# Two PSUM banks for the sums of y, with delta prepared in the one that is free, in a selective-scan kernel

## The chip, the cores and the metric

The kernel runs on one core of a Trainium2 chip. The metric is device time in microseconds, from the first to the last instruction of the program, as the median of several runs. An engine's share in the profile is taken over the span of one profiled execution, 5538.9 us.

## The reference

The input x is 4 images of 64 x 64 positions with 96 channels. Two layers run over it. Layer 0 normalises x in groups of three channels, projects it with signs only (weights and activations are replaced by their sign) to 192 channels xc and 192 channels z, runs a 3 x 3 convolution on the signs of xc, and applies SiLU; the result u has 192 channels and L = 4096 positions. Then comes a selective scan in K = 4 directions (rows, columns, and both backwards) with 16 states for each channel:

```python
x_dbl = jax.vmap(bilinear, ...)(xin, Wl, sl, bl)             # for each direction: dt (6), B (16), C (16)
dts = jax.vmap(bilinear, ...)(dts_in, Wd, sd, bd)            # 6 signs -> 192 channels
delta = jax.nn.softplus(delta + delta_bias)
def step(h, inp):
    ut, dt, Bt, Ct = inp
    dA = jnp.exp(dt[..., None] * A[None])
    h = dA * h + (dt * ut)[..., None] * Bt[:, :, None, :]
    y = jnp.einsum('bkdn,bkn->bkd', h, Ct)
    return (h, y)
```

The four directions of y are added, normalised over the channels, multiplied by SiLU(z) and projected with signs back to 96 channels. Layer 1 is attention without a softmax (so it collapses into small matrices summed over the image) and a feed-forward block with values rounded to 8-bit floats. What counts for this change is delta (softplus of a small projection), the scan, and the sum over the 16 states.

## The kernel before, in words

**Pieces.** The scan is cut into 1536 pieces (`Scans.pieces`): image b (4), direction e (4, in the order `KORD`), chunk ci of 1024 positions (4), group g of 32 channels (6), and quarter q of the 16 states (4). A piece is a tile of 128 partitions (32 channels x 4 states) by 1024 positions in float32. Its work, by engine:

- ScalarE, `decay` (L1231): dA = exp(delta x A), written into PSUM. There are two such tiles (pool `dA`, two banks each).
- GpSimd, `inject`: w = (delta x u) x B, four pieces ahead (`AHEAD`). The pool `w` has nine tiles.
- VectorE, `scan`: one scan instruction along the 1024 positions. It writes h over dA in PSUM or, if GpSimd is to make the product, into a tile `h` in SBUF.
- VectorE or GpSimd: the product h x C, over w. Which of the two is decided as the program is made: `Tally` adds up an estimate of each engine's work and `scan` gives the product to the one with less.
- ScalarE, `carry` (L1271): the last column of h is kept for the next chunk.
- TensorE, `reduce` (L1302, L1307): the sum over states, as a matmul with a constant of ones (`sum4`); eight pieces (two groups of channels) share one PSUM bank, tag `y`. With the last quarter of a group, earlier directions are added with a permutation (`back4`) or u with a diagonal (`dskip`).
- ScalarE, `evacuate` (L1316): copies the bank of sums to SBUF after eight pieces, and four stores follow.

**Order of a step.** The program is written in the order in which it is to run on each engine; no scheduler moves it. What is still chosen as it is built is which buffer of a pool a tile gets. In step i of `Scans.run` come: loads, carry(i-1), in every eighth step (i = 3 modulo 8) evacuate(i-4), decay(i+1), reduce(i-3), inject(i+4), a product that GpSimd still owes, scan(i), stores that are due (`Later.tick`), one stage of a preparation of delta, and one stage of the background work (`back`: the prologue of a later image, and the epilogue of an earlier one). Every engine works through its own queue in this order.

**Delta.** `prepare` makes softplus for 512 positions of 128 channels: eight small matmuls into a PSUM bank (tag `dps`), on ScalarE |t| and relu(t) (L1172, L1173), exp and ln (L1175, L1176) back into the same bank, a matmul that adds relu(t) (L1179), on VectorE the product with u, and on ScalarE a copy to SBUF (L1185). The results go to DRAM and come back, repeated over the states, with `load_dl`. One preparation begins in every eighth step, i = 0 modulo 8, and its stages lie in steps 0 to 5: matmuls; |t| and relu; exp and ln; relu added; product; copy. Three preparations run before the first scan, in tiles that the loop doesn't use yet.

**PSUM.** The eight banks are: four for the two dA tiles, one for sums of y, one for delta, two (`b0`, `b1`) for the background.

**Prologue.** For the group normalisation, the sums of x over all positions come from 64 matmuls, each with a tile of x (128 positions x 96 channels) as the weights and one column of ones moving (L510). The sums stand on 96 partitions, as the next matmul (`grp`, L516) needs them.

Of the kernel before, what the change touches and what calls it, by code (L numbers as in the profile page):

```python
# [53 lines left out]
def hybrid_kernel(ctx: ExitStack, tc: tile.TileContext, a: dict, out: bass.AP):  # L54
# [102 lines left out]
    def weights():  # L157
# [28 lines left out]
        def transposed(dst, srcs):  # L186

            count[0] += 1
            ps = p.ps.tile([128, 1024], BF16, name=f"tps{count[0]}", tag=("y", "dps")[count[0] % 2])
            at = 0  # L190
            for src in srcs:
                n, f = src.shape
                nc.tensor.transpose(ps[:f, at : at + n], src, identb[:n, :n])
                at += n
            nc.vector.tensor_copy(dst, ps[:f, 0:at], saturate=False if dst.dtype == F8 else None)
# [152 lines left out]
        nc.vector.tensor_copy(  # L348
            back4.rearrange("p (x d) -> p x d", x=4), ident.rearrange("p (x d) -> p x d", x=4)[:, ::-1, :]
        )  # L350
        ps = p.ps.tile([128, 512], F32, name="tpd", tag="dps")
        for g in range(3):
            for x in range(4):
                nc.tensor.matmul(
# [122 lines left out]
def prologue(c, b, xts=None):  # L477
# [5 lines left out]
    def f32(nm):  # L483
        return p.f.tile([128, 512], F32, name=f"{nm}_{b}", tag="f")
# [4 lines left out]
    with tc.tile_pool(name=f"xg_{b}", bufs=1) as xgp:  # L489
# [3 lines left out]
        with tc.tile_pool(name=f"cv_{b}", bufs=1) as cvp:  # L493
# [6 lines left out]
            if xts is None:  # L500
# [4 lines left out]
                load_x(c, b, xts)  # L505
                yield
                yield
            csum = bank("csum", 0)[0:96, 0:1]
            for i in range(NT):
                nc.tensor.matmul(csum, xts[i // 8][:, i % 8, :], c.ones1, start=(i == 0), stop=(i == NT - 1))  # L510
                if i % 8 == 7:
                    yield
            cs = f32("cs")[0:96, 0:1]
            nc.scalar.copy(cs, csum)
            gsum = bank("gsum", 1)[0:96, 0:1]
            nc.tensor.matmul(gsum, c.grp, cs, start=True, stop=True)  # L516
            yield
            negm = f32("negm")[0:96, 0:1]
# [578 lines left out]
class Scans:  # L1097
# [19 lines left out]
    def done(self, b, n):  # L1117

        return self.at > (b * NK + n) * NPC + SETTLE


    def load_signs(self, b, k):

# [6 lines left out]
    def prepare(self, spare=None):  # L1130

        nc, c, p = self.c.nc, self.c, self.c.p
        b, k, ci, part = self.todo.pop(0)
        nm = f"{b}_{k}_{ci}_{part}"

        at = 16 * (NCH - 1 - ci if k >= 2 else ci)
        if (b, k) not in self.gs:  # L1140
            self.load_signs(b, k)
        if (ci, part) == (NCH - 1, 0) and k != KORD[-1]:
            self.load_signs(b, KORD[KORD.index(k) + 1])
        ud = (c.utd if k % 2 else c.ud)[b].rearrange("h p (n l) -> (h p) n l", l=IW)
        if part != 1:
            u = spare[2] if spare else p.pu.tile([128, CH], F32, name=f"pu_{nm}", tag="pu")
            if part == 0:
                cuts = ((slice(0, 128), slice(0, 128), slice(at, at + 16)),)
            else:
                lines = [slice(at + 8 * x, at + 8 * x + 8) for x in range(2)]  # L1150
                cuts = [
                    (slice(64 * x, 64 * x + 64), slice(128, DN), lines[1 - x if k >= 2 else x]) for x in range(2)
                ]
            n = 16 if part == 0 else 8
            v = u[:, 0 : 64 * n].rearrange("p (n l) -> p n l", l=IW)
            for rows, chans, lines in cuts:
                nc.sync.dma_start(v[rows], ud[chans, lines])
            self.us = v[:, ::-1, ::-1] if k >= 2 else v
        gT = self.gs[b, k]
        uv = self.us[:, 8 * part : 8 * part + 8] if part < 2 else self.us  # L1160
        d = spare[0] if spare else p.pd.tile([128, 2, 512], F32, name=f"pd_{nm}", tag="pd")
        ps = spare[3] if spare else p.ps.tile([128, 512], F32, name=f"dps_{nm}", tag="dps")
        pv = ps.rearrange("p (c q s) -> p s q c", q=4, s=8)
        groups = ((0, 128, 0, part),) if part < 2 else ((0, 64, 128, 0), (64, 64, 128, 1))
        wd, c0 = (c.wdz, 32 * ci + 16 * part) if part < 2 else (c.wdy, 32 * ci)
        for s in range(8):
            nc.tensor.matmul(pv[:, s], wd[:, k, s], gT[:, :, c0 : c0 + 16], start=(s == 0), stop=(s == 7))  # L1167
        yield
        kind = part // 2
        sc, bi = c.pvd[:, kind, k : k + 1], c.dbias[:, kind, k : k + 1]  # L1170
        t = spare[1] if spare else p.pd.tile([128, 512], F32, name=f"sp_{nm}", tag="sp", bufs=1)
        nc.scalar.activation(d[:, 0], ps, AF.Abs, scale=sc, bias=bi)  # L1172
        nc.scalar.activation(t, ps, AF.Relu, scale=sc, bias=bi)  # L1173
        yield
        nc.scalar.activation(d[:, 0], d[:, 0], AF.Exp, scale=-1.0)  # L1175
        nc.scalar.activation(ps, d[:, 0], AF.Ln, bias=1.0)  # L1176
        yield

        nc.tensor.matmul(ps, c.ident, t, start=False, stop=True, skip_group_check=True)  # L1179
        yield  # L1180
        c.vec.tensor_tensor(
            d[:, 1].rearrange("p (i j) -> p i j", j=64), ps.rearrange("p (i j) -> p i j", j=64), uv, ALU.mult
        )
        yield
        nc.scalar.copy(d[:, 0], ps)  # L1185
        for x, (r0, n, d0, hf) in enumerate(groups):
            at = CH * ci + 512 * hf
            dst = c.dld[k][b][:, d0 : d0 + n, at : at + 512].rearrange("t d l -> d t l")
            then = (lambda: self.loaded.add((b, k, ci, part))) if x == len(groups) - 1 else None
            c.later.store(dst, d[r0 : r0 + n], after=1, then=then)  # L1190


    def load_bc(self, w, to, b, e, ci, q):
# [99 lines left out]
    def reduce(self, i):  # L1293

        c = self.c
        b, e, ci, g, q = self.pieces[i]
        if i % 8 == 0:
            self.ydone[i // 8] = c.p.ps.tile([128, 2, 256], F32, name=f"yp_{i}", tag="y")
        y, prod = self.ydone[i // 8], self.ins.pop(i)
        more = self.sums.pop(i // NQ, []) if q == NQ - 1 else []  # L1300
        for x in range(4):
            c.nc.tensor.matmul(  # L1302
                y[32 * x : 32 * x + 32, g % 2, :], c.sum4, prod[:, 256 * x : 256 * x + 256],
                start=(q == 0), stop=(q == NQ - 1 and not more), tile_position=(0, 32 * x),
            )
        for n, (src, w) in enumerate(more):
            c.nc.tensor.matmul(y[:, g % 2, :], w, src, start=False, stop=(n == len(more) - 1))  # L1307
# [15 lines left out]
    def run(self, back):  # L1323
        c, lanes, n = self.c, [], len(self.pieces)

        w = [c.p.w.tile([128, CH], F32, name=f"w_s{x}", tag="w") for x in range(7)]
        ps = [c.p.dA.tile([128, CH], F32, name=f"dA_s{x}", tag="dA") for x in range(2)]
        for x in range(3):
            half = slice(512 * (x % 2), 512 * (x % 2) + 512)
            lanes.append(  # L1330
                self.prepare((
                    w[x].rearrange("p (t l) -> p t l", t=2), w[3 + x // 2][:, half], w[5 + x // 2], ps[x // 2][:, half],
                ))
            )
        interleave(lanes)
        for q in range(NQ):
            self.load_bc(0, self.bt, 0, 0, 0, q)
            self.load_bc(1, self.ct, 0, 0, 0, q)
        while lanes:
            interleave(lanes)  # L1340
            c.later.tick()
        c.later.flush()
        self.load_dl(0)
        for m in (1, 2):
            self.load_dl(m)
        self.decay(0)
        for i in range(AHEAD):
            self.inject(i)
        for i in range(n):
            self.at = i  # L1350
            self.loads(i)
            if i % NQ == 1:
                while KORD[self.pieces[i][1]] == 2 and self.pieces[i][0] not in c.turned:
                    next(back)
                self.load_sums(i)
            if i >= 1:
                self.carry(i - 1)
            if i % 8 == 3 and i > 8:
                self.evacuate(i - 4)
            if i + 1 < n:  # L1360
                self.decay(i + 1)
            if i >= 3:
                self.reduce(i - 3)
            if i + AHEAD < n:
                self.inject(i + AHEAD)
            self.late_product()
            self.scan(i)
            c.later.tick()
            if i % 8 == 0 and self.todo:
                while (self.todo[0][0], self.todo[0][1] % 2) not in c.ready:  # L1370
                    next(back)
                lanes.append(self.prepare())
            interleave(lanes)
            next(back, None)
            if i > n - 64:
                next(back, None)
        self.late_product()
        for i in range(n - 3, n):
            self.reduce(i)
        self.evacuate(n - 1)  # L1380
        c.later.flush()
        self.at = 2 * n
# [76 lines left out]
```

## Time and profile before

Three runs took 5533.6, 5537.85 and 5543.78 us; the median is 5537.85.

| | busy us | share of the span | instructions |
|---|---|---|---|
| VectorE (DVE) | 5052.4 | 91% | 3237 |
| GpSimd (POOL) | 4994.2 | 90% | 2262 |
| ScalarE (ACT) | 3556.7 | 64% | 5564 |
| TensorE matmul (PE) | 3432.7 | 62% | 20197 |

The first scan starts 269 us after the first instruction and the last ends at 5421 us. In between, a piece takes 3.35 us on the mean. One scan takes VectorE 2.34 us and one product 1.23 us; a product takes GpSimd 2.35 us. A decay takes ScalarE 1.12 us.

How to read a line of groups: the line of the kernel, engine and operation, the tile written and those read, shapes and count; then busy us and mean ns of one; then the idle time of the engine just before such instructions, and what ended it. Line 401 is the helper that counts work, so there a group is told by its tiles. In a timeline each line is the start in us, how long it took, the engine, the line and the operation; in brackets stands how long the engine was idle before it and which instruction released it. Waits are listed as "who <- for whom: us in total, times, longest".

### The profile page before, as it was taken

The numbers are of one execution on the slowest core, as the hardware profiler recorded it, in microseconds if no ns is written. First come the engines' busy times: TensorE is split into PE (matmuls) and PEld (weight loads), VectorE is DVE, ScalarE is ACT, GpSimd is POOL, SyncE is SP. The second block draws the span as 40 slices with busy tenths as digits, with TensorE's granted clock in tenths as the row PEclk, the third lists the DMA queues.
The fourth block names the chain that finished last, engine by engine and source line by source line (L and its number), as shares of the span: only waits on it lengthen the run. The fifth ranks groups of instructions, "written<-read, shape, count | busy, mean of one in ns | idle before, by whom it ended". The sixth has DMA issues, their size and how long they took to land. (4 is left out here: it accounts for less than half of the span.)

```text
span 5538.9 us, 62371 instructions
## 1 busy us (share of the span) xinstructions
PE 3432.7 (62%) x20197; PEld 1356.7 (24%) x20197; DVE 5052.4 (91%) x3237; ACT 3556.7 (64%) x5564; POOL 4994.2 (90%) x2262
## 2 busy tenths in 40 slices
PE   6456665576557766577656766544676564444677
PEld 3222222222223222222222222211232121111223
DVE  3299999999999999899999999999999999999984
ACT  4467776777666667677766666755556775555554
POOL 2199999999999999899999999999999999999981
PEclk8667776678767876667777777766787766566778
DMA  4456666866766566666656566665666665665652
GB/s 78 118 179 198 207 194 193 258 193 199 220 203 194 194 205 199 218 217 207 205 193 212 185 200 210 212 211 191 210 215 186 191 205 198 205 208 190 207 159 60
DMA packets 613244, 1069.93 MB, mean 193 GB/s; under 512 B 225083, under 2 KB 343924, under 8 KB 611124
## 3 DMA queue, kind: packets, MB, share of 16 engines
q1 hardware_dynamic: 599428, 1065.88, 61.4%
q8 instruction: 159, 2.61, 0.2%
q10 hardware_dynamic: 13488, 0.07, 0.1%
q14 instruction: 169, 1.38, 0.1%
HBM read 833.20 MB, written 229.38 MB: 192 GB/s over the span
## 5 line engine op out<-in xcount | busy, mean ns | idle before, releaser
L401 POOL TENSOR_TENSOR w<-dl,bc 128x1024 f32<-128x1024 f32 x1536 | 3579.9, 2356 | 166.7 <-PE yp L1302 93.2
L1231 ACT ACTIVATE dA<-dl,anm 128x1024 f32<-128x1024 f32 x1536 | 1715.6, 1117 | 477.0 <-DVE w L401 291.5
L1302 PE MATMUL yp<-w,sum 128*32 128x256 f32 x12288 | 1261.6, 507 | 1083.2 <-ACT ys L1316 621.9
L401 DVE TENSOR_TENSOR_SCAN dA<-dA,cy,w 128x1024 f32<-128x1024 f32 x706 | 1654.4, 2343 | 94.7 <-ACT dA L1231 83.4
L401 POOL TENSOR_TENSOR w<-h,bc 128x1024 f32<-128x1024 f32 x596 | 1402.6, 2353 | 93.7 <-DVE h L401 85.2
L401 DVE TENSOR_TENSOR w<-dA,bc 128x1024 f32<-128x1024 f32 x940 | 1151.4, 1225 | 47.7 <-DVE dA L401 0.5
L401 DVE TENSOR_TENSOR_SCAN h<-dA,cy,w 128x1024 f32<-128x1024 f32 x446 | 1043.3, 2340 | 9.2 <-ACT dA L1231 8.7
L1302 PEld LDWEIGHTS yp<-w,sum 128*32 128x32 f32 x12288 | 308.0, 127 | 2136.9 <-issue 705.4
L1271 ACT COPY cy<-dA 128x1 f32<-128x1 f32 x707 | 110.8, 157 | 692.0 <-DVE w L401 690.7
L401 DVE TENSOR_TENSOR_SCAN dA<-dA,w 128x1024 f32<-128x1024 f32 x234 | 534.2, 2283 | 22.3 <-ACT dA L1231 18.0
L577 PE MATMUL cv<-tp,cw 96*96 96x512 fp8e5 x1152 | 359.9, 456 | 85.6 <-ACT r L627 70.5
L401 DVE TENSOR_TENSOR_SCAN h<-dA,w 128x1024 f32<-128x1024 f32 x150 | 341.8, 2279 | 24.4 <-POOL w L401 23.6
L1179 PE MATMUL dps<-sp,ident 128*128 128x512 f32 x378 | 356.8, 1043 | 0.0
L1307 PE MATMUL yp<-ya,back 128*128 128x256 f32 x576 | 237.8, 534 | 0.0
L577 PEld LDWEIGHTS <-cw 96*96 96x96 fp8e5 x1152 | 159.0, 146 | 277.5 <-issue 223.8
L1271 ACT COPY cy<-h 128x1 f32<-128x1 f32 x445 | 82.7, 186 | 145.6 <-DVE h L401 144.5
L847 PE MATMUL yc<-eys,mean 96*96 96x512 f32 x240 | 134.6, 713 | 33.3 <-DMA eys<-yd 14.5
L1307 PEld LDWEIGHTS yp<-ya,back 128*128 128x128 f32 x576 | 123.9, 248 | 127.8 <-issue 97.1
L1172 ACT ACTIVATE pd<-dps,dbias,pvd 128x512 f32<-128x512 f32 x189 | 143.8, 761 | 16.4 <-PE dps L1167 13.0
L1173 ACT ACTIVATE sp<-dps,dbias,pvd 128x512 f32<-128x512 f32 x189 | 144.7, 766 | 0.0
L401 DVE TENSOR_TENSOR pd<-dps,pu 128x512 f32<-128x512 f32 x189 | 127.6, 675 | 4.6 <-DMA dl<-dld 4.3
L1316 ACT COPY ys<-yp 128x512 f32<-128x512 f32 x192 | 111.7, 582 | 30.2 <-PE yp L1307 24.3
(282 smaller groups left out, 4017.6 us busy)
## 6 DMA issues: line engine op xcount, KB each, us to landing
dl<-dld SPq DMA_DIRECT2D x768, 512.0 KB
bc<-bcd SPq DMA_DIRECT2D x512, 512.0 KB
dld<-pd SPq DMA_DIRECT2D x126, 512.0 KB
yd<-ys SPq DMA_DIRECT2D x768, 64.0 KB
dld<-pd SPq DMA_DIRECT2D x126, 256.0 KB
ya<-yd SPq DMA_DIRECT2D x192, 128.0 KB
pu<-ud SPq DMA_DIRECT2D x32, 512.0 KB
pu<-utd SPq DMA_DIRECT2D x31, 512.0 KB
```

The costliest lines, as they stand in the source:

```text
L401: return getattr(self.eng, name)(out, *args, **kw)
L577: nc.tensor.matmul(ps, c.cw[:, j, t, 96 * h : 96 * h + 96], tpad[j][:, 8 * q + dy : 8 * q + dy + 8, dx : dx + IW], start=(j == 0 and t == ...
L847: self.c.nc.tensor.matmul(ps, w, x, start=(i == 0), stop=(i == len(pairs) - 1))
L1172: nc.scalar.activation(d[:, 0], ps, AF.Abs, scale=sc, bias=bi)
L1173: nc.scalar.activation(t, ps, AF.Relu, scale=sc, bias=bi)
L1179: nc.tensor.matmul(ps, c.ident, t, start=False, stop=True, skip_group_check=True)
L1231: c.nc.scalar.activation(t, self.dlt[i // NQ][0], AF.Exp, scale=c.anm[:, g, NQ * KORD[e] + q : NQ * KORD[e] + q + 1])
L1271: self.c.nc.scalar.copy(self.carries[g, q], h[:, CH - 1 : CH])
L1302: c.nc.tensor.matmul(y[32 * x : 32 * x + 32, g % 2, :], c.sum4, prod[:, 256 * x : 256 * x + 256], start=(q == 0), stop=(q == NQ - 1 and no ...
L1307: c.nc.tensor.matmul(y[:, g % 2, :], w, src, start=False, stop=(n == len(more) - 1))
L1316: c.nc.scalar.copy(t, y[:, :, ::-1] if k >= 2 else y)
```

## The change

There are five edits. The bank `dps` is given up, and the sums of y have two banks, `y0` and `y1`, in turn. A preparation of delta uses whichever of the two does not collect sums at the time (`bank`). For that it begins in steps 4 modulo 8, when the other bank has just been evacuated, and has to be done by step 10, as in step 11 (3 modulo 8) that bank takes new sums. Second, its ScalarE operations are spread out, one a step: matmuls; |t|; relu; exp; ln; relu added; product and copy, in steps 4 to 10. Third, in a step the decay now stands ahead of the evacuation. Fourth, as the preparations begin later in their eight steps, a fourth one runs before the first scan, and a store of delta is issued two ticks after it was asked for instead of one. Fifth, the sums of x are made with the ones as the weights, which stand, and four tiles of x (384 columns) moving: 16 matmuls, then a copy of the row, and four small matmuls that turn it onto 96 partitions while adding its four parts.

```diff
-            csum = bank("csum", 0)[0:96, 0:1]
-            for i in range(NT):
-                nc.tensor.matmul(csum, xts[i // 8][:, i % 8, :], c.ones1, start=(i == 0), stop=(i == NT - 1))
-                if i % 8 == 7:
+            csum = bank("csum", 0)[0:1, 0 : 4 * DM]
+            for i in range(0, NT, 4):
+                nc.tensor.matmul(
+                    csum, c.ones1, xts[i // 8][:, i % 8 : i % 8 + 4, :].rearrange("p i e -> p (i e)"),
+                    start=(i == 0), stop=(i == NT - 4),
+                )
+                if i % 8 == 4:
                     yield
+            row = f32("csr")[0:1, 0 : 4 * DM]
+            nc.scalar.copy(row, csum)
+            ps = bank("cst", 1)[0:96, 0:1]
+            for i in range(4):
+                nc.tensor.matmul(
+                    ps, row[:, DM * i : DM * i + DM], c.ones1[0:1, :], start=(i == 0), stop=(i == 3)
+                )
+            yield
             cs = f32("cs")[0:96, 0:1]
-            nc.scalar.copy(cs, csum)
...
+    def bank(self):
+        return max(0, self.at - 3) // 8 % 2
...
-        ps = spare[3] if spare else p.ps.tile([128, 512], F32, name=f"dps_{nm}", tag="dps")
+        ps = spare[3] if spare else p.ps.tile([128, 512], F32, name=f"dps_{nm}", tag=f"y{1 - self.bank()}")
...
         nc.scalar.activation(d[:, 0], ps, AF.Abs, scale=sc, bias=bi)
+        yield
         nc.scalar.activation(t, ps, AF.Relu, scale=sc, bias=bi)
         yield
         nc.scalar.activation(d[:, 0], d[:, 0], AF.Exp, scale=-1.0)
+        yield
         nc.scalar.activation(ps, d[:, 0], AF.Ln, bias=1.0)
         yield
...
         c.vec.tensor_tensor(
             d[:, 1].rearrange("p (i j) -> p i j", j=64), ps.rearrange("p (i j) -> p i j", j=64), uv, ALU.mult
         )
-        yield
         nc.scalar.copy(d[:, 0], ps)
...
-            c.later.store(dst, d[r0 : r0 + n], after=1, then=then)
+            c.later.store(dst, d[r0 : r0 + n], after=2, then=then)
...
-            self.ydone[i // 8] = c.p.ps.tile([128, 2, 256], F32, name=f"yp_{i}", tag="y")
+            self.ydone[i // 8] = c.p.ps.tile([128, 2, 256], F32, name=f"yp_{i}", tag=f"y{i // 8 % 2}")
...
+        u = c.p.pu.tile([128, CH], F32, name="pu_s", tag="pu")
+        for _ in self.prepare((w[7].rearrange("p (t l) -> p t l", t=2), w[4][:, 512:CH], u, ps[1][:, 512:CH])):
+            pass
...
+            if i + 1 < n:
+                self.decay(i + 1)
             if i % 8 == 3 and i > 8:
                 self.evacuate(i - 4)
-            if i + 1 < n:
-                self.decay(i + 1)
...
-            if i % 8 == 0 and self.todo:
+            if i % 8 == 4 and self.todo:
```

## The prediction, made before the result

> **What bounds the kernel now.** I read the page's table of engines first, then the same table for three stretches: up to the first scan, the loop over the 1536 pieces, and the tail.
>
> ```profile
> ## 1 busy us (share of the span) xinstructions
> PE 3432.7 (62%) x20197; PEld 1356.7 (24%) x20197; DVE 5052.4 (91%) x3237; ACT 3556.7 (64%) x5564; POOL 4994.2 (90%) x2262
> ...
> 0.00:269.00 269.00, 151.29 (x745) 87.85 (x746) 75.59 (x137) 121.16 (x198) 42.28 (x104) 0.79 0.44 95
> 269.00:5423.00 5154.00, 3200.21 (x19184) 1232.58 (x19183) 4925.79 (x3006) 3383.21 (x5278) 4948.66 (x2154) 0.71 0.64 201
> 5423.00:5539.00 116.00, 81.25 (x268) 36.26 (x268) 50.99 (x95) 52.31 (x88) 3.22 (x6) 0.78 0.22 64
> ```
>
> After the stretch and its length the columns are PE, weight loads, DVE, ACT, POOL. In the 5154 us of the loop VectorE is busy 4926 us and GpSimd 4949 us: both are nearly full, and the change alters the work of neither. Both programs, built, put 940 products on VectorE and 596 on GpSimd. What can move is idle time, so the next view is who VectorE waits for in the loop.
>
> ```profile
> DVE dA L401 <- ACT dA L1231: 101.3, 86, 5.5
> DVE h L401 <- POOL w L401: 23.6, 2, 14.4
> DVE g L401 <- PE sy L847: 19.7, 9, 4.6
> DVE h L401 <- ACT dA L1231: 9.3, 9, 3.1
> DVE dA L401 <- ACT cy L1271: 8.9, 12, 1.3
> ```
>
> Columns: total us, times, longest. All VectorE waits of the loop are 173 us (a further 54 us are gaps under 150 ns); 119.5 of them are for ScalarE (101.3 + 9.3 + 8.9), nearly always for the next decay. GpSimd as a releaser is two waits at the start. So **VectorE sets the time, and ScalarE's lateness is its only large wait.** GpSimd's own waits (93.6 us for sums, 85.2 us for scans) are slack while VectorE doesn't wait for it. The timeline shows how a decay comes late:
>
> ```profile
> 2412.25 2.34 DVE L401 TENSOR_TENSOR_SCAN h<-dA,cy,w 128x1024 f32<-128x1024 f32 x1
> 2412.73 0.15 ACT L1271 COPY cy<-dA 128x1 f32<-128x1 f32 x1
> 2414.62 1.12 ACT L1231 ACTIVATE dA<-dl,anm 128x1024 f32<-128x1024 f32 x1 [1.74 <-DVE h L401]
> ...
> 2415.84 2.36 DVE L401 TENSOR_TENSOR_SCAN dA<-dA,cy,w 128x1024 f32<-128x1024 f32 x1 [1.25 <-ACT dA L1231]
> ...
> 2418.26 0.58 ACT L1316 COPY ys<-yp 128x512 f32<-128x512 f32 x1
> ...
> 2418.74 1.12 ACT L1231 ACTIVATE dA<-dl,anm 128x1024 f32<-128x1024 f32 x1
> ...
> 2419.96 2.36 DVE L401 TENSOR_TENSOR_SCAN dA<-dA,cy,w 128x1024 f32<-128x1024 f32 x1 [0.43 <-ACT dA L1231]
> ```
>
> Two kinds. First, the decay at 2414.62 was given the PSUM banks that the running scan still reads, though the other pair was free; it starts when that scan ends, and VectorE then stands 1.25 us. Second, the decay at 2418.74 stands behind the evacuation at 2418.26. The built program says how often the first happens: 73 decays lie in the banks of the piece just ahead. Numbering the trace's scans in order, VectorE idles 84.9 us before those 73 (1.16 each). Of the other idle for ScalarE (37.7 us), 16.2 us fall on pieces 4 modulo 8, whose decay follows an evacuation, 4.7 on pieces 3 modulo 8, about 10 on pieces 0 modulo 8, where ScalarE waits for squares of the epilogue.
>
> **What the Trainium skill says.** (1) "PSUM — Partial Sum Buffer", section Engine vs sequencer instructions: ScalarE's and VectorE's queues are strict FIFO. The trace agrees: at 2412.9 ScalarE has ready work behind the decay and sits 1.74 us. (2) Same page, PSUM bank collisions raise a hardware error: instructions of different engines on one bank are kept apart by a dependency, a read from a read too. The trace agrees: the carry copy, which needs only the scan, waits 690.7 us in all for the product that reads the same tile. (3) "Perfetto Trace Analysis", Optimization Strategy: a repeating bubble on the full engine can mean too little PSUM for the next tile; the 1.25 us is one. (4) Same page, Optimizing Scalar/DVE Operations: breaking up work on an unsaturated engine that causes bubbles elsewhere may help. That speaks for the change; ScalarE is 66% busy in the loop (3383/5154).
>
> **The change part by part.** The rows that price it:
>
> ```profile
> L401 DVE TENSOR_TENSOR pd<-dps,pu 128x512 f32<-128x512 f32 x189 | 127.6, 675 | 4.6 <-DMA dl<-dld 4.3
> L1316 ACT COPY ys<-yp 128x512 f32<-128x512 f32 x192 | 111.7, 582 | 30.2 <-PE yp L1307 24.3
> L1185 ACT COPY pd<-dps 128x512 f32<-128x512 f32 x189 | 109.2, 578 | 3.7 <-DVE pd L401 3.7
> L510 PE MATMUL csum<-ones,xt 128*96 128x1 f32 x256 | 42.6, 297 | 18.2 <-DMA xt<-in_x 18.2
> ```
>
> (a) Decay ahead of the evacuation, one ScalarE operation of delta a step. Both take work out from in front of a decay. At most the 16.2 and 4.7 us above go; nothing else in the 37.7 us comes from these operations. I take -21.
>
> (b) The copy of delta now stands in the same step as the VectorE multiplication, where before a step lay between. They read one bank, so the copy waits for the multiplication, and the multiplication runs after that step's scan and product. Queued behind the copy are the step's background operations, a carry copy and the decay of piece 4 modulo 8, for which VectorE waits next. From the start of the multiplication: it ends after 0.7, copy 0.5, background B, carry 0.2, decay 1.1, 0.1 to the scan: 2.6 + B. VectorE needs that decay after 0.6 + 2.25 = 2.85 if piece 3 modulo 8 has its product on GpSimd, 4.0 if not. So the stall is B - 0.23 or B - 1.38. The built program has 188 such copies in the loop; 102 of the pieces after them have their product on GpSimd (before, pieces 3 modulo 8 had 68, as the load count that picks the engine sees the multiplication first). Pairs of background operations (B near 1.1 to 1.3) are common. Summing B by the rows' means over the built order, less what falls together with (c), gives 17 us in 35 places. Bounds: 0 (ScalarE always early) and 50 (other lateness adds). I take +17.
>
> (c) Which banks a decay gets. In the changed program 91 decays lie in the banks of the piece just ahead instead of 73; the 18 more are nearly all at 4 modulo 8 (28 against 11). 18 x 1.16 = +21. Bounds 0, if ScalarE would have been late there anyway, and 18 x 1.7 = 31 (the mean at 1 modulo 8).
>
> (d) Two banks for sums. TensorE's first matmul of eight waited 621.9 us in all for the evacuation. It now waits for the copy of (b), in the bank that delta just used, and that copy ends about 0.5 us later in the step than the evacuation did. So this wait is renamed, not removed. Behind it are TensorE's sums and background matmuls; GpSimd waits for the sums to give buffers back, VectorE does not wait for GpSimd. I take 0; a bound of +30 if GpSimd's waits grow by a third and reach VectorE.
>
> (e) Start. A fourth delta is prepared before the loop: 3 us of ScalarE and a multiplication that waits for a load queued behind six others, and the first decay queues behind its copy. I expect the first scan up to 6 us later. It is hidden: GpSimd's six first products run from 266.6 to 280.4, and the third scan waits 9.2 us for GpSimd anyway. One multiplication less in the loop: -0.7. Column sums: 64 matmuls took 10.3 us (32.7 to 43.0, clock 1.00). The 16 new ones move 384 columns; a float32 matmul of 512 columns has two passes, and eight such passes in a row took 3.67 us at full clock with 0.59 us for one, so 0.44 apart ((3.67 - 0.59)/7); 384 columns give 0.33, and 16 x 2 x 0.33 = 10.6. Nothing is won; a row copy, four small matmuls and one more step come after: +1.5 on the path to the first scan. For images 1 to 3 this lies in the background.
>
> Longer lead of the delta store and the other bank tags: nothing, as VectorE waits for that load only once (4.3 us).
>
> Sum: -21 + 17 + 21 + 0 - 0.7 + 1.5 = +19, so 5538 + 19 = **5557 us**.
>
> **The rivals.** *Smoother ScalarE pays (5512).* (b) is hidden and the 18 extra bank clashes fall where ScalarE is late anyway; then -21, and 5 of the remaining 17 us go too: -26. For: ScalarE has a third of its time free. Against: the built order puts the copy between two decays. *It cancels (5538).* Gains of (a) against half of (b) and (c). For: the three terms are of one size. Against: nothing in particular. *GpSimd becomes the bound (5585).* (d) lengthens its waits so far that injections reach VectorE late; +30 and the +19. For: 93.6 us of such waits now. Against: four pieces of lead, and no such VectorE wait after the start.
>
> **How the numbers follow.** Main case (5545 to 5575) 0.45, faster 0.20, cancelling 0.25, GpSimd 0.10. Slower by over 0.2% means above 5549: all of GpSimd's and nearly all of the main case, 0.55; within 0.2% 0.25; faster 0.20. For eight in ten I go from 5510 (just below the faster rival) to 5592 (both upper bounds partly in).
>
> **What would show it.** VectorE's waits for the decay rise from 119.5 to about 140 us, gathered on pieces 4 modulo 8; the copy of delta waits for the multiplication on ScalarE (3.7 us before) by over 100 us; TensorE's wait for the evacuation turns into one for that copy of about the same total; VectorE's busy time stays within 5 us; the first sum group (third scan) starts within 4 us of 282.8. The prediction is wrong if the waits before scans fall under 100 us, or if GpSimd shows up as a releaser of scans beyond the start.

## The result, and the profile after

The changed kernel takes 5563.18 us, the median of four runs (5557.92 to 5568.8); the kernel before took 5539.91 us in four runs (the three above and one more). The ratio is 1.0043, 95% interval 1.0026 to 1.0061: slower by 23 us, a small loss, but one that the measurement tells from nothing.

The table of engines of the changed kernel comes first, with two groups from the list of costly ones.

```profile
PE 3508.2 (63%) x20037; PEld 1353.2 (24%) x20037; DVE 5054.7 (91%) x3237; ACT 3546.9 (64%) x5568; POOL 4996.7 (90%) x2262
...
L1319 PE MATMUL yp<-w,sum 128*32 128x256 f32 x12288 | 1320.2, 525 | 806.8 <-ACT pd L1202 343.2
...
L1202 ACT COPY pd<-dps 128x512 f32<-128x512 f32 x188 | 110.2, 586 | 445.9 <-DVE pd L401 445.9
```

The first of these two groups in the kernel before (the second stands in the prediction, as L1185):

```profile
L1302 PE MATMUL yp<-w,sum 128*32 128x256 f32 x12288 | 1261.6, 507 | 1083.2 <-ACT ys L1316 621.9
```

VectorE's and GpSimd's busy times have moved by 2.3 and 2.5 us (5052.4 and 4994.2 before), ScalarE's by 10. TensorE's rose by 75 us with fewer instructions; a sum took 507 ns and now takes 525, on an engine that is 63% busy. So the 23 us are not work of a full engine but idle time between its instructions. The copy of delta (L1202) is what stands out: it takes about as long as before, 586 ns (578 before), but ScalarE now stands 445.9 us in front of it, where it stood 3.7.

Next, VectorE's waits in the loop of the changed kernel (total us, times, longest).

```profile
DVE dA L401 <- ACT dA L1248: 104.1, 93, 3.0
DVE w_s L401 <- DMA pu_s<-utd: 20.4, 1, 20.4
DVE h L401 <- ACT dA L1248: 15.2, 18, 2.2
...
DVE dA L401 <- ACT cy L1288: 9.7, 7, 2.1
DVE pd L401 <- PE dps L1197: 8.7, 3, 4.8
```

The three rows for ScalarE give 104.1 + 15.2 + 9.7 = 129.0 us (119.5 before). The rows for TensorE grew too, so these three alone are not the whole difference. For that I cut the time in three at the third scan and at the last one, and within the loop added up all of VectorE's waits over 150 ns:

| us | third scan starts | loop, third scan to last | VectorE's waits in it | loop without them | last scan to the end |
|---|---|---|---|---|---|
| before | 282.8 | 5138.7 | 163.7 | 4975.0 | 117.4 |
| after | 276.3 | 5164.2 | 188.3 | 4975.9 | 122.5 |
| difference | -6.5 | +25.5 | +24.6 | +0.9 | +5.1 |

The loop grew by 25.5 us, and VectorE's waits in it by 24.6. In all kernels below the loop without its waits stays between 4965 and 4978 us, so VectorE's waits are what every experiment changes. The last column lies between 117.4 and 122.8 us in all thirteen kernels (122.5 in e1, 117.7 in e6, which differ only in the order of a step), so its 5.1 us are not put down to the change.

By the engine that the profile names as the releaser, ScalarE has 126.3 us of these waits before and 137.6 after, TensorE 26.6 and 40.1. So about half of the added waiting is for TensorE, 8.7 us of it in three waits for the matmul that adds relu to delta (the last row above), for which VectorE did not wait at all before.

Where the waits fall, by numbering the scans ("idle at 4 modulo 8" is VectorE's idle time in front of the scans of pieces 4, 12, 20 and so on): 73 pieces lay in the PSUM banks of the piece just ahead (a bank clash, below), with 84.9 us of idle in front of their scans; now 91 do, with 102.9 us. All other scans at 4 modulo 8 had 16.2 us and now have 9.1; those at 3 modulo 8 fell from 4.7 to 1.1.

On TensorE the first of eight sums waited 621.9 us for the evacuation (L1302 above). In the changed kernel that wait has two names:

```profile
PE yp L1319 <- ACT pd L1202: 343.2, 101, 6.3
...
PE yp L1319 <- ACT cy L1288: 117.9, 33, 6.0
```

Together 461 us, a quarter less.

At the start, the timeline of the changed kernel shows the fourth delta in front of the first scans.

```profile
268.43 0.69 DVE L401 TENSOR_TENSOR w_s<-dA_s,pu_s 128x512 f32<-128x512 f32 x1 [20.37 <-DMA pu_s<-utd]
269.15 0.59 ACT L1202 COPY w_s<-dA_s 128x512 f32<-128x512 f32 x1 [16.77 <-DVE w_s L401]
...
270.87 4.47 DVE L401 TENSOR_TENSOR_SCAN h<-dA,w 128x1024 f32<-128x1024 f32 x2 [1.74 <-ACT dA L1248]
276.33 2.29 DVE L401 TENSOR_TENSOR_SCAN h<-dA,w 128x1024 f32<-128x1024 f32 x1 [1.00 <-POOL w L401]
```

VectorE stands 20.4 us for the load of u, the first scan starts at 270.9 instead of 269 us, and the third one waits a last microsecond for GpSimd, where it waited 9.2: the delay is hidden, as GpSimd's first products still end later than it, but little room is left.

### The profile page after: what moved, and what is told of

Same layout as the page of the kernel before. It is cut to its first block, busy times and chain, and to the rows that moved or that the text cites. A ratio compares the mean times of both kernels' runs of the same rounds, so it can differ in the third digit from the quotient of the medians.

```text
span 5563.1 us, 61882 instructions
## 1 busy us (share of the span) xinstructions
PE 3508.2 (63%) x20037; PEld 1353.2 (24%) x20037; DVE 5054.7 (91%) x3237; ACT 3546.9 (64%) x5568; POOL 4996.7 (90%) x2262
## 5 line engine op out<-in xcount | busy, mean ns | idle before, releaser
L401 POOL TENSOR_TENSOR w<-dl,bc 128x1024 f32<-128x1024 f32 x1536 | 3583.3, 2362 | 161.0 <-PE yp L1319 81.9
L1319 PE MATMUL yp<-w,sum 128*32 128x256 f32 x12288 | 1320.2, 525 | 806.8 <-ACT pd L1202 343.2
L401 DVE TENSOR_TENSOR_SCAN dA<-dA,cy,w 128x1024 f32<-128x1024 f32 x705 | 1652.3, 2344 | 97.8 <-ACT dA L1248 78.5
L1197 PE MATMUL dps<-sp,ident 128*128 128x512 f32 x376 | 343.7, 1012 | 233.5 <-ACT dps L1194 233.5
L1202 ACT COPY pd<-dps 128x512 f32<-128x512 f32 x188 | 110.2, 586 | 445.9 <-DVE pd L401 445.9
L1324 PE MATMUL yp<-ya,back 128*128 128x256 f32 x576 | 215.4, 491 | 1.2 <-DMA ya<-y 1.1
L1197 PEld LDWEIGHTS dps<-sp,ident 128*128 128x128 f32 x376 | 85.3, 283 | 369.9 <-ACT dps L1194 310.1
L1183 PE MATMUL dps<-gT,wdz 128*128 128x64 fp8e5 x1000 | 117.8, 320 | 41.1 <-DMA gT<-gTd 21.2
```

What stands on the lines that cost most here:

```text
L401: return getattr(self.eng, name)(out, *args, **kw)
L1319: c.nc.tensor.matmul(y[32 * x : 32 * x + 32, g % 2, :], c.sum4, prod[:, 256 * x : 256 * x + 256], start=(q == 0), stop=(q == NQ - 1 and no ...
```

## The experiments

Two things had to be taken apart: whether the loss comes from the extra bank clashes (term c of the prediction) or from the copy behind its multiplication (term b), and whether the parts meant as gains (terms a and d) gain anything. Each ratio is to the kernel before, run beside it on the same chip. There were three batches (e1 to e4, e5 to e8, e9 to e11), in which the kernel before took 5540.8, 5536.5 and 5538.7 us, so a difference of medians between two batches holds up to 4 us that belong to no edit. The last column is from one profiled execution of each kernel (163.7 us before, 188.3 in the changed kernel).

| label | built from | what is different | us | ratio, 95% interval | VectorE's waits in the loop, us |
|---|---|---|---|---|---|
| e1 | before | dA tiles take turns | 5485.1 | 0.9902 (0.9887 to 0.9917) | 117.0 |
| e2 | after | dA tiles take turns | 5501.7 | 0.9937 (0.9924 to 0.9949) | 124.4 |
| e3 | e2 | multiplication a step ahead of the copy | 5455.7 | 0.9850 (0.9836 to 0.9863) | 88.9 |
| e4 | e2 | evacuation ahead of the decay | 5527.1 | 0.9974 (0.9965 to 0.9983) | 150.0 |
| e5 | e3 | one ScalarE operation a step again | 5446.7 | 0.9840 (0.9825 to 0.9854) | 82.1 |
| e6 | e1 | decay ahead of the evacuation | 5489.7 | 0.9913 (0.9900 to 0.9927) | 122.3 |
| e7 | after | multiplication a step ahead of the copy | 5508.9 | 0.9951 (0.9938 to 0.9963) | 139.1 |
| e8 | before | new column sums | 5539.8 | 1.0008 (1.0000 to 1.0017) | 160.7 |
| e9 | e2 | sums and delta each in one bank | 5516.4 | 0.9955 (0.9943 to 0.9968) | 138.9 |
| e10 | e5 | sums and delta each in one bank | 5457.8 | 0.9854 (0.9839 to 0.9869) | 95.4 |
| e11 | e1 | copy in the step of its multiplication | 5494.3 | 0.9921 (0.9907 to 0.9934) | 122.5 |

**The bank clashes: e1 and e2.** The two dA tiles get a tag each, so that a piece can't be given the banks of the piece ahead: 73 and 91 clashes become none (the few other users of the pool get one of the two tags as well). Nothing else of the order changes. The same edit was made on the kernel before (e1) and on the changed one (e2).

```diff
-dA=pool("dAp", 2, space=PSUM)
+dA=pool("dAp", 1, space=PSUM)
...
-        t = c.p.dA.tile([128, CH], F32, name=f"dA_{i}", tag="dA")
+        t = c.p.dA.tile([128, CH], F32, name=f"dA_{i}", tag=f"dA{i % 2}")
```

> The kernel before, with the two dA tiles forced to take turns (a tag for even pieces, one for odd), so that no decay gets the banks that the running scan reads; before, 73 did. Theory A (VectorE's wait for a late decay is the time, and a bank clash costs it 1.16 us): the 85 us of idle before those scans go, so 5540 becomes 5455 to 5480, and VectorE's waits for decays in the loop fall from 119 to 25 to 50 us. Theory B (a clash falls where ScalarE is late anyway, or GpSimd's waits for sums set the time): little or nothing, 5525 to 5545.

> The changed kernel with the same forced turns (91 clashes to none). Theory A: 103 us of idle go, so 5563 becomes 5460 to 5485, and against the kernel before with forced turns it is within 10 us, because what then remains of the change is -21 for the earlier decay and the split, +17 for the copy behind the multiplication. Theory B: stays at 5550 to 5565. Theory C (the sums' wait on the copy of delta is the loss): still 20 to 30 us above the kernel before with forced turns.

Measured: -54.8 us on the kernel before, -61.5 on the changed one: a clear gain in both, but e1 stays above the 5480 and e2 above the 5485 us that theory A allowed, and e2 is 16.6 us above e1, not within 10. VectorE's waits for decays in e1 are 64.6 us, not 25 to 50. The gap was not for lack of PSUM, as point (3) of the prediction took it: the same two tiles, in turns, do without it. In the kernel before 84.9 us stood in front of the clashing scans and 49.7 in front of all others, 134.6 together; in e1 78.5 us are left. So 29 of the 85 us came back as other lateness, most of it at 1 modulo 8 (2.1 us at scans without a clash, now 15.4) and 4 modulo 8 (16.2, now 22.7). A clash is worth 54.8/73 = 0.75 and 61.5/91 = 0.68 us, not the 1.16 us that stand in front of it in the trace. By the medians the extra clashes of the changed kernel cost 61.5 - 54.8 = 6.7 us; by VectorE's waits (188.3 - 124.4 less 163.7 - 117.0) they cost 17.2. The first is a difference of three ratios, each known to 7 to 10 us either way, and the second rests on one execution of each kernel, so their cost stays open between nothing and some 20 us. What is left between the two kernels without clashes, 16.6 us, must come from the other edits.

**The copy behind its multiplication: e3 and e7.** The multiplication goes one step ahead of the copy again; to keep the copy in step 10, |t| and relu share a step. On e2 (e3), and on the changed kernel as it is (e7).

```diff
         nc.scalar.activation(d[:, 0], ps, AF.Abs, scale=sc, bias=bi)
-        yield
         nc.scalar.activation(t, ps, AF.Relu, scale=sc, bias=bi)
...
             d[:, 1].rearrange("p (i j) -> p i j", j=64), ps.rearrange("p (i j) -> p i j", j=64), uv, ALU.mult
         )
+        yield
         nc.scalar.copy(d[:, 0], ps)
```

> The changed kernel with forced turns, and the copy of delta one step behind its multiplication again (for which |t| and relu(t) share a step as before). If the copy behind the multiplication costs the predicted 17 us: 10 to 20 us less than the changed kernel with forced turns, and ScalarE's wait for the multiplication before that copy (446 us) falls under 50. If it costs nothing: within 5 us of it, or slower because the sums now wait a step longer for the bank.

> The changed kernel as it is (buffers chosen as built), with only the copy of delta put one step behind its multiplication and |t| and relu(t) in one step. Its build has 65 bank clashes instead of 91. With forced turns this step took 46 us off. Theory A: 40 to 60 us off 5563, so 5503 to 5525, which is faster than the kernel before; VectorE's waits fall from 189 to about 140. If the copy behind the multiplication costs only the 17 us predicted: 5530 to 5545 with the 26 clashes.

Measured: e3 is 46.0 us faster than e2, e7 54.3 us faster than the changed kernel (e7 also has 65 clashes instead of 91, an estimated 18 us at the 0.7 us above, so e3 is the cleaner of the two). For e3 10 to 20 us were expected; e7 is as expected, VectorE's waits in it too (139.1 us). ScalarE's wait for the multiplication falls from 449.5 us in e2 to 1.6 in e3. One edit of two lines takes the changed kernel from slower than before to faster. The same place of the program in both traces shows how. First e2, ScalarE and then VectorE, at the piece where three background operations (B = 1.8 us) follow the copy:

```profile
1969.01 0.59 ACT L1202 COPY pd<-dps 128x512 f32<-128x512 f32 x1 [2.87 <-DVE pd L401]
1969.49 0.59 ACT L1082 CAST h<-hp 128x512 f16<-128x512 f32 x1
1970.11 0.72 ACT L1083 ACTIVATE h<-h,b1q 128x512 f16<-128x512 f16 x1
1970.74 0.61 ACT L1085 ACTIVATE h<-h 128x512 fp8e5<-128x512 f16 x1
1971.26 0.14 ACT L1288 COPY cy<-dA 128x1 f32<-128x1 f32 x1
1971.43 1.12 ACT L1248 ACTIVATE dA<-dl,anm 128x1024 f32<-128x1024 f32 x1
```

```profile
1968.29 0.68 DVE L401 TENSOR_TENSOR pd<-dps,pu 128x512 f32<-128x512 f32 x1
1968.89 2.34 DVE L401 TENSOR_TENSOR_SCAN h<-dA,cy,w 128x1024 f32<-128x1024 f32 x1
1972.64 2.36 DVE L401 TENSOR_TENSOR_SCAN dA<-dA,cy,w 128x1024 f32<-128x1024 f32 x1 [1.41 <-POOL w L401]
```

ScalarE has nothing to do for 2.87 us, because its queue is headed by a copy that has to wait. Then it has 3.5 us of work before the decay is done (1969.01 to 1972.55), and VectorE could use that decay 2.3 us after the end of the multiplication, when the scan in between ends. The bracket names GpSimd as the last releaser, but the decay ends at 1972.55 and the scan starts at 1972.64: it is the decay that came last. Now e3, ScalarE at the same piece:

```profile
1943.42 1.12 ACT L1248 ACTIVATE dA<-dl,anm 128x1024 f32<-128x1024 f32 x1
1944.47 0.58 ACT L1202 COPY pd<-dps 128x512 f32<-128x512 f32 x1
1944.95 0.58 ACT L1082 CAST h<-hp 128x512 f16<-128x512 f32 x1
...
1946.80 1.11 ACT L1248 ACTIVATE dA<-dl,anm 128x1024 f32<-128x1024 f32 x1
```

```profile
1945.96 2.33 DVE L401 TENSOR_TENSOR_SCAN dA<-dA,cy,w 128x1024 f32<-128x1024 f32 x1
```

The copy goes right behind the decay, and VectorE's scan of that piece has no idle in front of it. Over the loop, idle at 4 modulo 8 falls from 30.6 to 6.3 us; VectorE's waits for delta's relu matmul fall from 9.5 to 0.7, idle at 2 modulo 8 from 9.8 to 2.4; at 3 modulo 8 it rises from 2.5 to 12.3. The edit also moves exp, ln, the relu matmul and the multiplication one step earlier, so not all of the 46 us need come from the copy's wait: what stands behind the copy, at 4 modulo 8, is 24 us.

**The same term in the kernel before: e11.** On e1 the step between multiplication and copy is taken out.

```diff
             d[:, 1].rearrange("p (i j) -> p i j", j=64), ps.rearrange("p (i j) -> p i j", j=64), uv, ALU.mult
         )
-        yield
         nc.scalar.copy(d[:, 0], ps)
```

> The kernel before with dA tiles that take turns (5485.1 us) and one more edit: the copy of delta in the step of its multiplication (steps 4 modulo 8 instead of 5). This is the second term of the prediction alone. By the prediction's size: 5502. By the size that the changed kernel showed (46 us): 5525 to 5535, ScalarE's copy waiting some 400 us for the multiplication, VectorE's idle gathered behind it. Rival (in the kernel before ScalarE's step has room there, and the cost comes only with the other edits): 5485 within 6 us.

ScalarE's waits in e11:

```profile
ACT pd L1184 <- DVE pd L401: 408.5, 186, 6.7
```

ScalarE's wait is nearly as long as in the changed kernel (445.9), and yet the kernel is only 9.2 us slower than e1, by the medians (the intervals overlap). The idle behind the copy is there: at 6 modulo 8, whose decay follows the copy here, it rises from 4.8 to 25.1 us. But the other scans lose 6.5 us of idle (73.7 to 67.2) and other instructions of VectorE 8, so that all its waits in the loop grow by 5.5 us only. So the stall itself has the size of e3's at 4 modulo 8 (20 and 24 us); what becomes of it depends on what else is late. Of the sizes expected of the whole, the 46 us of e3 is excluded here; neither the predicted 17 us nor no cost at all fits the medians well, but the intervals exclude neither. In the changed kernel the late copy also holds up the decays and TensorE's work of the steps next to the evacuation; which of these accounts for the rest of the 46 us was not taken apart.

**Decay ahead of the evacuation: e4 and e6.** Taken back on e2 (e4, below), and done alone on e1 (e6, the same lines the other way round).

```diff
-            if i + 1 < n:
-                self.decay(i + 1)
             if i % 8 == 3 and i > 8:
                 self.evacuate(i - 4)
+            if i + 1 < n:
+                self.decay(i + 1)
```

> The changed kernel with forced turns, and the evacuation ahead of the decay as before (edit 3 undone). If that order was worth the predicted 16 us: 5 to 16 us slower than the changed kernel with forced turns, with the new idle of VectorE on pieces 4 modulo 8. If ScalarE has time there now that delta is spread: within 5 us.

> The kernel before with forced turns, and of the change only the decay ahead of the evacuation. VectorE idles 22.7 us on pieces 4 modulo 8 in the kernel before with forced turns (5485). Theory A: most of it goes, 5462 to 5475. If the wait of the sums for the evacuation mattered more (the evacuation comes 1.1 us later in the step): the same or slower, 5480 to 5500.

In the changed kernel the order is worth 25.4 us, more than the 5 to 16 expected: without it idle at 4 modulo 8 is 54.6 us instead of 30.6. In the kernel before it is worth nothing (5489.7 against 5485.1, with intervals that overlap), which was the second of the two expectations. There idle at 4 modulo 8 does fall, from 22.7 to 10.3 us, but with one bank for the sums the evacuation now comes a decay later, and the sums wait for it: 763.7 us on TensorE where e1 has 586.7. Delta's matmul stands behind the sums, so VectorE waits for that:

```profile
DVE pd L401 <- PE dps L1179: 18.0, 14, 5.0
```

In e1 that wait is 4.4 us. So the gain of 12 us on one wait is given back by others. That it is the single bank which makes the difference between e4 and e6 is read from these waits; no run of one bank with the order of e4 shows it.

**Two banks for the sums: e9 and e10.** Sums always in one bank and delta always in the other, as before; on e2 (e9) and on e5 (e10).

```diff
-tag=f"y{1 - self.bank()}"
+tag="y1"
...
-tag=f"y{i // 8 % 2}"
+tag="y0"
```

> The second kernel of these experiments (the changed one with dA tiles that take turns, 5501.7 us) with the two banks' turns taken back: sums of y always in one bank, delta always in the other, as in the kernel before; every other edit stays. Theory of the prediction (the second bank only renames TensorE's wait): 5502 within 10 us, the wait of the first sums named after the evacuation again, about 600 us. Rival one (the second bank is what makes the decay ahead of the evacuation harmless): the sums wait for an evacuation that is now behind the decay, delta's matmul queues behind them, 5515 to 5530. Rival two (the sums suffer from waiting for the late copy, which no longer gates them here): 5475 to 5490.

> The fastest kernel so far (5446.7 us: turns for the dA tiles, the copy one step behind its multiplication, one ScalarE operation a step) with sums always in one bank and delta always in the other. If the second bank is worth nothing by itself: 5447 within 8 us. If it is what lets the decay go ahead of the evacuation: 5465 to 5485, with VectorE's waits for delta's matmul on TensorE above 10 us (0.7 in the kernel with the late copy).

TensorE's longest wait in e9 is again that for the evacuation:

```profile
PE yp L1319 <- ACT ys L1333: 813.0, 165, 9.2
```

Without turns TensorE's wait for the evacuation is 813.0 us in e9 and 820.1 in e10, where e2 has 328.3 us for the copy of delta and 124.4 for a carry copy. The time grows by 14.7 and by 11.1 us; each pair's intervals just overlap, but both point one way, and VectorE's waits in the loop grow by 14.4 and 13.3 us. By the ratios, which take out the differences between batches, it is 10 and 8 us. So e9 falls in the range of its first rival and e10 between its two expectations. Neither goes the way that was expected: VectorE's wait for delta's matmul stays at 8.0 us in e9 (9.5 in e2) and at 0.9 in e10. What rises is GpSimd's wait for sums to free its buffers (66.3 us in e2, 100.3 in e9; 47.0 in e5, 64.7 in e10) and idle at 6 modulo 8 (4.7 and 16.4; 9.7 and 19.4); how the one leads to the other is not shown. So the second bank is worth some 8 to 15 us once the decay goes ahead of the evacuation: probably more than a renaming, but not what everything hangs on.

**One ScalarE operation a step: e5.** On e3, |t| and relu each get a step again, and a preparation begins one step earlier to have time for both.

```diff
         nc.scalar.activation(d[:, 0], ps, AF.Abs, scale=sc, bias=bi)
+        yield
         nc.scalar.activation(t, ps, AF.Relu, scale=sc, bias=bi)
...
-            if i % 8 == 4 and self.todo:
+            if i % 8 == 3 and self.todo:
```

> The changed kernel with forced turns of the dA tiles, the copy of delta one step behind its multiplication, and still one ScalarE operation of delta a step: the preparation begins one step earlier, in steps 3 modulo 8, right after the evacuation of that bank. Theory A (late decays are the time): the 12 us of idle that came on pieces 3 modulo 8 in the variant where |t| and relu(t) share a step go, so 5440 to 5455. If one operation a step is worth nothing by itself: 5456 within 5 us.

9.0 us less than e3 by the medians and 5.5 by the ratios, with intervals that overlap. VectorE's waits in the loop fall from 88.9 to 82.1 us, which agrees with it. But the idle at 3 modulo 8 that was to go falls only from 12.3 to 10.2 us, and at 6 modulo 8 it rises from 1.9 to 9.7; what is gained lies at 1 and 5 modulo 8 and in front of VectorE's other instructions. Most likely a small gain; it is not shown beyond doubt. This kernel beats both: 1.6% less than the kernel before, and by the medians 116 us less than the changed one. It has all five edits of the change, with the multiplication a step ahead of its copy and the dA tiles in turns.

**Column sums alone: e8.** The diff is that of the change (its first part), on the kernel before.

> The kernel before with only the column sums of x made the new way; its build has 75 bank clashes (before 73). Expected: 5532 to 5548, with the bias for the signs of x ready at 45 us as before (7.6 us of matmuls for 10.3, but a copy, small matmuls and a step more). If standing ones are a gain of their own: ready 3 us earlier.

No difference (1.0000 to 1.0017). The 64 matmuls took 10.34 us and the 16 new ones take 7.48, but the row copy and the four small matmuls after them take the 3 us back: in the kernel before the value that the image waits for (`negm`) comes 12.4 us after the first of these matmuls (32.7 to 45.1 us), in e8 12.9 (31.4 to 44.3).

## Why the prediction was right

Direction and size were right: +19 us forecast, +23 measured, all of it in VectorE's waits. The place was right in part: the forecast had the loss in waits for late decays on ScalarE, and about half of it is in waits for TensorE. That the sum came so near is luck, for its terms missed by more than the sum did, in both directions. (As written they add up to +17.8, not +19.) With e1, e2, e6 and e9 the 23.3 us divide as follows, by the medians and by VectorE's waits in the loop:

| part | kernels compared | medians, us | VectorE's waits, us |
|---|---|---|---|
| extra clashes | before, e1, e2, after | +6.7 | +17.2 |
| decay ahead of the evacuation | e1, e6 | +4.7 | +5.3 |
| place and spread of the preparation, its copy, the fourth preparation, the later store, the column sums | e6, e9 | +26.7 | +16.5 |
| second bank in turns | e9, e2 | -14.7 | -14.4 |

The two columns agree on every sign, though +4.7 is within the noise; how much goes to the clashes and how much to the third row stays open. The fourth preparation and the later store were not run alone. The parts depend on the order in which they are put in, as e4 and e6 show.

- **(a), -21: right in the changed kernel, wrong as a term by itself.** The decay ahead of the evacuation is worth 25 us there (e4), but nothing in the kernel before, which has one bank for the sums (e6). I looked only at what stood in front of the decay, not at who waits for the evacuation that moves back. The spread over steps is worth up to 9 us, if anything (e5).
- **(b), +17: right mechanism, too small.** Up to 46 us in the changed kernel (e3, which moves other stages too), near the bound of 50; 9 in the kernel before (e11). At the place shown the formula holds: for three background operations it gives 1.77 - 0.23 = 1.54 us and the trace has 1.41. Its sum came out at 24 us (idle at 4 modulo 8, e2 against e3) for 17. What failed is that only the decay directly behind the copy was counted; delta's matmul and the scans at 2 modulo 8 were late as well.
- **(c), +21: right mechanism, probably too large.** 18 more clashes cost 6.7 us by the medians and 17.2 by VectorE's waits. The idle in front of a clashing scan (1.16 us) is not what it costs: without the clash part of the delay shows elsewhere, 29 of 85 us in e1. At the 0.7 us of a clash in e1 and e2, 18 of them would be 13 us (an estimate). Nor do the 18 lie at 4 modulo 8 alone: there are 17 more there, 8 more at 2 modulo 8 and 9 fewer at 3 modulo 8.
- **(d), 0: the wait was renamed as told**, to the copy and the carry copy, but it also got shorter (621.9 to 461 us), and turns between the banks were worth 8 to 15 us (e9, e10). The Trainium skill, "Perfetto Trace Analysis", section Optimizing Tensor Performance, advises turns between banks so that an evacuation can lie beside the next group's matmuls; the runs agree, within the limit that delta's copy now gates the bank (343.2 us of TensorE's wait).
- **(e), about 0: right.** The third scan came at 276.3 us, outside the 4 us around 282.8 that I named, but for another reason: the convolution of the first prologue ended at 184.1 us instead of 191.0, with a higher granted clock on its way (0.80 against 0.61 between 80 and 100 us). In all thirteen kernels the third scan starts 91.4 to 92.3 us after the end of that convolution, which lies between 183.3 and 191.0 us, so such differences of up to 8 us belong to no edit. The price of the column sums was too high (10.6 against 7.5 us): the profile has one record for each of the 16 matmuls, where I reckoned two passes each.

Of the signs: VectorE's wait for decays is 129.0, not about 140 us; all idle at 4 modulo 8, clashes counted in, rose from 31.2 to 38.1, and at 2 modulo 8 from 4.3 to 22.6, while at 3 modulo 8 it fell from 18.5 to 3.7; the copy's wait is 446 us (over 100 foretold); VectorE's busy time moved 2.3 us. The rivals: *Smoother ScalarE pays* is what one gets when the copy is moved (e7, ratio 0.9951); in the changed kernel as built (b) was not hidden. *GpSimd becomes the bound* is excluded by VectorE's waits: in the loop of the changed kernel 6.2 us of them are for GpSimd (3.3 before), and GpSimd's wait for sums fell from 93.6 to 81.9 us.

## What to carry to other kernels

On engines that work in order, an instruction that waits costs what is queued behind it, not its own wait: the copy of delta held ScalarE for about 450 and 409 us in two kernels, and taking that wait away won up to 46 and 9. Put a step between a producer on one engine and its consumer on another, and before moving work back (here an evacuation) ask who waits for it. When a pool of two tiles is meant to be a double buffer, read from the built program which tile each use gets; forcing turns was worth 1% here, more than all that the change was about.

## What the runs showed of the hardware that was not expected

The 16 new matmuls of the column sums started 0.64 us apart and, from 4.8 us after the first one, 0.32 apart, while the granted clock in the profile was 1.00 in both stretches. In the two lines below, of the changed kernel, the columns are the stretch, its length, these matmuls, their weight loads and the granted clock; the last two are of the DMA.

```profile
32.00:36.80 4.80, 4.69 (x8) 0.97 (x9) 1.00 0.27 54
36.90:39.50 2.60, 2.60 (x9) 0.59 (x7) 1.00 0.69 35
```

The Trainium skill, "TensorE: Matmul & The Clock Gate", Part 1, tells of a half clock until the engine has been busy for at least one window of some 3.4 us, which does not begin with the first matmul but runs freely. The factor of two agrees, and 4.8 us is not against it; the profile's clock doesn't show it. That it was this gate is not shown by any run here.
